# A four-layer graph network on one core: a tile turned through DRAM in layer 3, a recurrent step split by graph, another order of the tasks and dummy products

## The chip, the cores and the metric

The kernel runs on one core of a Trainium2 chip. The metric is the time of one execution on the device in microseconds (us), the median of the runs shown. The engines that matter are TensorE (PE, with its weight loads PEld), VectorE (DVE), ScalarE (ACT), GpSimd (POOL), and SyncE (SP), whose queue issues every DMA of this kernel.

## What is computed

64 graphs of 256 nodes with 256 features pass four residual layers, each `x = x + layer(relu(layernorm(x)), adj)`. All numbers are float32; the adjacency is int32.

```
layer 0  q, k, v = h@Wq, h@Wk, h@Wv in 8 heads of 32
         softmax(where(adj > 0, q@k.T / sqrt(32), -1e9)) @ v, then @Wo + bo
layer 1  Wh = h@W;  e = leaky_relu(Wh@a1 [:,None] + Wh@a2 [None,:])
         attention = softmax(where(adj > 0, e, -9e15), axis=1);  elu(attention @ Wh)
layer 2  three times:  m = h@weight[i];  aggr = A.T-sum of m over the edges
         h = GRU(aggr, h):  r, z = sigmoid(...);  n = tanh(i_n + r*h_n);  h = (1-z)*n + z*h
layer 3  f = h@W.T + b in 4 heads of 64
         logits = leaky_relu(s_src[i] + s_dst[j]), masked where adj != 1
         out = softmax(logits, over j) @ f
```

## The kernel before

**Tiling.** The graphs are taken two at a time, 32 pairs. A pair's x lives in one tile of 128 partitions x 1024 (four chunks of 128 nodes x 256 features: two per graph), loaded at the start and stored after layer 3. Six such x tiles exist, so several pairs are under way at once. Other working tiles come from pools with fixed numbers of slots (`SLOTS`, L324): 21 tiles "w4" of 4 KB per partition, 5 "w2" of half that size, 8 PSUM banks "ps", 8 DRAM tiles "turn" of 512 KB, 4 "turn2" of 256 KB.

**The order of the work.** Nothing runs in the order in which it is written. Each piece of work is a `Task` with one or more forms (an engine, an estimated time, and the instructions); `Plan.add` (L195) notes which tiles it reads and writes. A constant string `ORDER` (L48) holds, for every task, a rank and the form chosen. `Plan.order` (L240) sorts the tasks by rank, walks through them once with a small model of the engines (when each is free, how long a result takes to reach another engine, `latency` times 1.4 for a DMA), gives each tile the slot that comes free first, and emits the instructions. Every engine then works through its own list in that order, waiting for semaphores. Changing an estimate changes the slots given out; changing `ORDER` changes each engine's list. The planner also charges 0.19 us when TensorE changes the mode of its array: "full" 128x128, "rows" of 32 (layer 0's scores, L844), "columns" of 32 (layer 0's context, L896), and "halves" of 64 columns (layer 3's product, L1300).

**Transposes.** Layers 0, 2 and 3 need the normalized tile with features on partitions. `norm_relu` (L584) has two ways. One uses TensorE: eight transposes of 128x128 into two PSUM banks (L664), each bank then passed through relu to SBUF by ACT (L676) or DVE (L677). The other, `turn_rows` (L764), goes through DRAM: one DVE transpose of 32x32 blocks over the whole tile (L768), a store of 512 KB to a "turn" tile (L723) and four loads of 128 KB that bring the blocks back in turned places (L726), then relu from SBUF (L648 on ACT, L649 on DVE). `by_dma` (L580) decides: layers 0 and 2 go through DRAM for pairs 0 to 30, and so do the three results of layer 2's steps ("2m", L1199); layer 3 and the last pair use TensorE. Apart from that, the exponentials of layers 0 and 3 are turned through DRAM by `turn` (L732), except in layer 3 of the last pair (`turn_keys`, L737).

**Layer 2.** Each of three steps computes gates with 512-column products for both graphs of a pair at once (`gate`, L1117; the products at L1124): the new part of h (L1134, L1136), the messages along the edges (L1101), then reset, update and candidate (L1149, L1154, L1163, L1172, L1176) and the new state (L1181, L1187, L1192).

**Layer 3.** The features f come from TensorE (L1246); destination scores go through DRAM to all partitions (`to_all`, L923, its DMAs at L928 and L936); ACT forms the logits (L1277), DVE masks them and finds the row maximum (L792), ACT takes the exponential (L799). After `turn`, the product with f (L1300) leaves the result with features on partitions. For all pairs but the last it is turned back by a DVE transpose (L1316), a store (L1320) and four loads (L1323), then scaled by the softmax sum and added to x by 16 DVE instructions of 64 columns per pair (L1334).

Of the kernel before, what the change touches and what calls it, by code (L numbers as in the profile page):

```python
# [11 lines left out]
FP = mybir.dt.float32  # L12
# [25 lines left out]
class Task:  # L38
    __slots__ = ("pair", "forms", "form", "bufs", "rank", "stage", "mode", "before", "end", "engine", "latency")


class Plan:
# [3 lines left out]
    SLOW, SWITCH = 1.4, 0.19  # L46

    ORDER = (  # L48
        "c-rlI2Y_T%m3Ezb?|b*<S2=f8=iJki6U>kqh9FVNf`bxFxW-*vcSZDHRM1_+qO7>AxQa?rRz*hQNQMbaf?;y%?&;}R)m{1B{}wPamAa>TNTS"
        "m)-PKk1y?fvJ&iT%F&b^JSGxS-RKJ<7U64EsK?}%Y0r__{_Uj7&8U+e;ezYbn~=5t^|8eRr>NB1*mH>9AK9{<I<U8uk53z1K3{?Urxi6f5Qp"  # L50
        "L85YtP5wZZ@SSCI;`VY0Agr<EfaDCgryJGK(Ao(E2C;o?=fQTkzr5V#aIKFa#Nd>s5>pHWbHM_>$|64w^(2_*j$qy`J@LNQq%PQK<`58FlP~"
        "$<JEDo{#ESp7_z7CW5ce#tL#Wpf@eThz7NR=y5@}0kspJe)|$O2>umFYylNhQC@e^E0f2Te%2str2(qFGNjvbbF{ERFq&#gcA0UPGtUekhbK"
        "zCz59hn_{m1x->~fk2lAxkK5COxG4=@6cgSv;5{*V21VINSEKmd^d+9c365cS8qMSiO%HR#X)9F3MmcZz7~N&rF#&^iobfD~eh`*egbjDW`9"
        "1wS{JiI^V?IT=JRjmdV)g^7hzpaA%lfSSNr6;c5exo0VTkD-*FLK(XqA;2x$VwXE4A>5x~^YO*0(Ns-Z8EHf?cZ}|Ro=W?iIjO%@f|j(N{lF"
        "^(Ajq;fOlUfYEj(+LOfBDnTFVj;Q&WGwgD4zb1BRd<TA*t~%`kGt2w)}I5IoJfU%t^TWxRn?#&#&*@MA(e$GCUezY|mvYHL7g>}m7T`VRq?#"
        "a<*~S1$!06|SaI?rJwi9ylkKX#1j1Nx0A@quIKznsS=L2V;Z&PAbFBXrLcJR&!}8hnz5uH%%izMqC^snY$s33X}lK3a9*;8%pV-Ifm4%U)_x"
        "!v(Fa)2us26bgfXND^Q&Nztg2Q0e*rn0&ExS>iPJmXFqv@0JYL4h{#cZeLy;qL^qH+&|oLB3o4(bHBDH6%#>CNU<?50oe=H?IHP%m{&@H_nZ"
        "U!II>@i49iv=xMzdVQQZPr%aX5Pe47jt9<K967n%TJDNE!Q04f)RNPi=lS*54@PpFx3^R4Cro4H!p<EG+`(kG?#Y#x`{+E@56gMjq1B2~Um>"
        "bqF<vnA2P!fE}x;HW0G22i)-3=_a^+bB?is>pKB%xbhS3JwgIokd=nuCI}6&&Ax2&dP5A1tLC}#hTzXcZCs_7tZCo=q^JUd=C(oC*T6n%8ke"
        "l>02SQmwaBj8y?YmI-Oo-${sA|cZ=hX2c7ss^i;+lfk^n^dkter)^oGs=fUqDf<R~)X?u#Y<38>t42()L!R9}>PAmd&|I8F%S5_f)-5l?-Dh"  # L60
        "zNyzG?6ue0|v;yvR{sGjh+DCUMk!Vu48L<gtn@n+2LLn%tQQ^-F`@1V4n%!mTJ&GEW6w)9)wf84MWY}hpwOlKU&`+=Hsd!$aq9~?Z*EmxNbW"
        "}4d8}Lc|f{Gr(f(`bdn@K8TNoL!f_gv$7g0_)-?i@A(G?PgII8f7!&FR<g#Zn2q`h7=op{d_{({ZZ%ub)(S|M+XrrXs*PX2+9Evlc1!_qgt1"
        "N4^fN*JYqxHw^+)ZQF>`gNP!a^=|`JZ(Jp`?-XA*O{X6Ysf{hbzpiM=U3@lODV5W2FAmzpmdASmznV=R^DE+SjmuuP@c4r)22Zeeu5Ub@~~?"
        "?XF?#y4iM4Blxnrq?Kv|GjWuXTq78Zmjg1#<4AR+hE#BgxJxi!c^SkERc5(gN+v+gh{B?{!5+mTr`nlW&UUy3?)->Zt14E*2sas;m&@c{nGF"
        "OIA_N3M=XUHRVaW4dbf*-h*xMkE+XF)5tU4i}eGDFeD?NS}UA;6ie#sLj-;SckImx#jALdsG!5O1z9yhu^EZ8Bgc)0mtx@5dG?~&On35~Yk?"
        "F!gM9<z(aSaPM`VK=2S>;4@+<k2B8WcR3$)L*hIH6ZQ<hbVYKoW(5Gy3c3vEP*g;+SJn8W8Vv=nD;WMBR)=q(rCi2DG=^R2tOZ`u`d=U5e%K"
        "_nCY6W0BIaaqb~4dlR*}F%^L;U6q}a)y=IN@pi3we8Z0LG>?T01z{DVb=4*B~j9&c!20@v9u>~*AW6BewH@h|1cg}N;J@f9C{!AFkQgxiD*$"
        "^PR{VU%;^LM{i!4CSluby__bCSfAK=2afJ8N-=;DgpgYhb?P!|-k0%3ShCn6qoY7u*g^kBPLqujZsW4Njo_^!j$Bbi!%7S>jhZY6DmRbnq-~"
        "8T193rCIK@nMo)Rs<m>kW;PXIh(EpLnpcC!zt^2;7X|ysyls-;6rqmN;Zt`lLa$yhyY6!GlVfZ2u;Jb2cYai<7jBZzGeEi@iRTfpli52xo+p"
        "&{<^jcNALBWy4%O_G!Q<XC>)EK_sz>()XwU^B@<(>bj`qDy?qQ1_gz15(DN+ow5ex5daGpS0y<i{+qiMOUP@`I+W1JIRy|Le;$3qtBaSR4H5"  # L70
        "%`l4Z73(Z`rLLAo$P(4?lwK`=;QymOM632FArVCoiCDNauCgucT&#$Oc(7WOpFyTHLhB+t_wJ~Mx>benLqMGTNjfhALPho{a)*qFN;XT^JY2"
        "6G)_8S|M(aLT<gE{(KDZG=w10WX~tUS5HmIXCa&3iDqMTN$8&4gx6enX^)_w0&t=5AP~)`q{u|VjWq@P$Ipqd|^?<<XkT&JU2fE-C9((J)Is"
        "AcUfO-ha%f`MK@c?|G@r==~$37|%oxtM8z%xJew!o~FZk`3zXm1D`F7T$6)m;LRv;>^1DVGJq;PnFO2}Sq04DPsw2->2ayUu-L*>d!0_&$6_"
        "KQlUa%MuWzo~4(cDMl2$&W~XM5?~IkA6gfldEz<&RFO)i7=g{r;PCf_*MZ%s;WhGff$&UQM`66F$qGG)&VomvGw4C}gbM|n)z%9TBJgZ&hzk"
        "?Dy*`OEjXn!wjVHc(f#HUv+=C<`?hr9}Swz$lNfRec19{UOj++A`qBF?>7xDZ-(bL9_4FO7%HK=p%%pod?BW@5H<8|=AZQ~S4!_*|uW@U}Jd"
        "l7~1G|EL#LTR<UDR-Q5N`g}?;JoLvesYcTl?8EbXn>VVVumyz%1B_rT~0^btDL;=WB>bK4qx1^EnD`$$+hNUJGf{6=ubn_p>3XN`Xt%>#_=~"
        "ogO1&ajE?0&o|Hs6{NE3D-uY`UH&X4Vnjd#v6Lt)@`>wg?L_CvpTE=lT$Bnx^;)9@Ag2iPA8t{W8hvgJ`_E?a(eDm`JZRh63+`lmQtrMOR^@"
        "JB@NIUHx+VYfd`KQ;ymy|iahgJF5Q`Ver@~4L11Py3GyLnCyK$|j68PjrbZ2MD9E=YhM1s$MZUEsm6O|@$vY*8EYet_%5Om?oYmrrvh{U7@h"
        "Wa^a5K)>A6^o*f}05-_bpnwkD3F4^Z+H~3`36M~?ql1``6b#r!IF2qWLib~hrV|aIv<y*rk~<p8<`it`UX*Zbx|)mD5KdWL(2-Mi1S~UY1ff"
        "M6VXN>^otOp7!8Ik2+*h99YBHS6Xda}a?=lZt@(2ZD_jmNj4p&x)|M{Axe#0LgG6ZRtWEu&3`_}wrLLNBv>%aK<@-OFQyz`Em(sRB8$OX0Xb"  # L80
        "@O&!Ot~T5|Mb!)@BK#WqYyE&-7iK#^QMLcZOo0nbl>^#DV3(@cs}w6?X$<}M$8KxYLfhCTcEE?s#~%m^V!g6?1~B|A~H#GNa`F&X3x#wD^2P"
        "E>017*`b$a&f5bFxe+AhSP8!{L#ohmsyAykS+dS98ciYb9(Rz*?)i_&`pPdE@5_fX-(F{~vl3L?-pFJXbLW0tVgg`A%b|A<gkpb+-3VL3F#a"
        "yXCV_L~6up62T>EiDxXL*q-D-yU#PJc}yDu&%Sn3v_GBc{n7k<r?I?g%D|cSVK(k(ixp3e3fUgDE6q5y3%t5N4!}){dZL2?-~HIx7U3d0bjH"
        "i76I^W{~<C2BiH>3ho?qXI8F{XofUMgNp8jl(zB=lV`M;f=nqx&&N(h5JcSpFwMPN2r%ixFJNVTU;`KN{l|`?1Y)yRaV?6lKsh>aT+6IqJ_#"
        "O%(SxzMXKV&JX_)8CdU);QrXDw;Id|a;D=zvRp3dD2h$hqyr;s!2Mvb1n@Ew%6Q1F=eDT#lqb7rU~p!$;EQd?hb^LFlR%bZpJQ+d>sM2VMHy"
        "gUF;3ri`FawSd21njU>iM#!_0QYWTT#F8ZD2k{y*#}E}PtVys{Ts7?3QwU1v=~15=n|7719!B#3>O+k5ah{?G@=vT4>?cpG2}vVZg;ndN4)N"
        "&D_OIiKrO&u8uh4(5%MII6#o?~_-x-T-t&l^>lr_hw9&vCMevHAN8G%kk`**Pi?xP~!AlC6uc%>2Z`k7=P-E`6EFjsB%^VPH5mj=)Y3t?8qg"
        "Ko%#k7p>hp2`9&s_%;HSu_Ag2qwBa@co^e9oE9baEw&#cJ7*)rwKn(nm&);qtDIi(jsV2q?tBR!}xUj0AhafX=w;gYM?7O)(I}O}hX16`GLd"
        "`a}drpUSC08gKsO!uh7iFw9vB|MQqs!`;xUWwL$w7$e8Ow(L{g>M!gaLU@1Np+mE^&!A}y2d+!}{tujkkZ|RS<DcAPkX#6K+`4Y9%;h+l&xV"
        "aNr~d$gF*gE7!eC64ozaXXuQ-;IdXjPp)R0d|J0+ejxb`{!ehG=l=Z*z-o|9RA`uf&w@J09`T#svRMtf_tI{uiSJ;|V9=ohgR;WA{7BfHn-o"  # L90
        "bDrta$Yf@2G{gc+Qd0<A2&0G7fhJN!PNqm6Vmp?9iM1yhDYI2MHb|g8;`XPcwX`wZa~l5L%IY8Ze$K6Xklf>dhCcdio1dyo+dCQ7B`0O$@-O"
        ")n2}OS0Bdz=L;r1h%qfl9ld>Y#&sgo+a221bCIvziHSmm<Fb8$FM4H|Gp%?L}WvKgne1+}tG|jbvB5Q&UKCYC1DtevZkxU*cjp`_BB52u_$N"
# [190 lines left out]
def tile_adj_preln_d4(  # L283
# [100 lines left out]
    def buf(tag):  # L384
        return Buf(tag, tiles[tag])

    def w4():
        return buf("w4")
# [1028 lines left out]
```

## Time and profile before the change

| what | value |
|---|---|
| time, median of 3 runs | 3501.86 us (3501.18 to 3503.47) |
| the profiled execution: its time | 3501.53 us |
| the profiled execution: span from first to last instruction | 3499.7 us |
| TensorE busy | 3433.5 us, 98% of the span |
| DVE busy | 3078.1 us, 88% |
| ACT busy | 2522.0 us, 72% |
| POOL busy | 453.1 us, 13% |
| DMA, the core's queue | 749.98 MB, 69.3% of 16 engines' span |
| gate products, L1124, two groups | 2304 instructions each, 1071.2 and 1064.9 us |
| granted TensorE clock, mean | 0.993 |

How to read it: the page gives busy time of each engine, the span in 40 slices with the busy share in tenths, the DMA queues, the chain of work that ended last, and the costliest groups of instructions by line. A float32 matmul is recorded as two instructions. Matmuls overlap in the records, so the distance between the starts of two groups says how long one holds TensorE, rather than the duration of one record.

### The profile page before, as it was taken

How to read it: one execution, taken by the hardware profiler on the slowest of the kernel's cores; microseconds unless marked ns; L12 is line 12 of the kernel's file. 1: busy time of each engine (PE TensorE's matmuls, PEld its weight loads, DVE VectorE, ACT ScalarE, POOL GpSimd, SP SyncE). 2: the span in 40 equal slices, each digit the busy share in tenths (PEclk: the TensorE clock that was granted, in tenths of full speed). 3: DMA queues.
4: the chain of work that ended last, by engine and by line, in shares of the span. 5: the costliest groups of instructions: out<-in, count | busy, mean ns of one | idle time of the engine just before them, and what ended most of it. 6: DMA issues, size and time to landing. Idle time of an engine off the chain costs nothing.

```text
span 3499.7 us, 53732 instructions
## 1 busy us (share of the span) xinstructions
PE 3433.5 (98%) x14784; PEld 1931.6 (55%) x14784; DVE 3078.1 (88%) x9047; ACT 2522.0 (72%) x6739; POOL 453.1 (13%) x497
## 2 busy tenths in 40 slices
PE   8899999999999999999999999999999999999997
PEld 5555555555555555555555555555555555555554
DVE  8788998999999989999899888999889989889767
ACT  7756786766776777777767777778777768668545
POOL 1010110111111111111111111111011111011010
PEclk9999999999999999999999999999999999999998
DMA  8655877777677777777776777777677776576444
GB/s 287 209 150 167 248 240 217 224 229 228 212 217 233 226 222 235 223 225 225 218 230 215 228 227 216 235 230 234 214 228 216 234 224 218 183 220 201 155 131 136
DMA packets 596081, 753.41 MB, mean 215 GB/s; under 512 B 99012, under 2 KB 507076, under 8 KB 595780
## 3 DMA queue, kind: packets, MB, share of 16 engines
q1 hardware_dynamic: 595780, 749.98, 69.3%
q8 instruction: 118, 1.93, 0.2%
q14 instruction: 183, 1.50, 0.1%
HBM read 426.78 MB, written 314.59 MB: 212 GB/s over the span
## 4 chain that ended last, share of the span: by engine, by line
PE 64%; DVE 7%; DMA 3%; ACT 2%; issue 1%; SPq 1%; POOL 0%; DVEq 0%; ACTq 0%; POOLq 0%
PE ps L1124 37%; PE ps L823 4%; PE ps L1101 4%; PE ps L1246 3%; PE ps L844 3%; PE ps L1300 2%; PE ps L699 2%; PE ps L1031 2%; PE ps L896 2%; PE ps L1017 2%; PE ps L911 2%; DMA w<-turn 2%; DVE w L792 1%; DVE w L954 1%; DVE x L1334 1%
## 5 line engine op out<-in xcount | busy, mean ns | idle before, releaser
L1124 PE MATMUL ps<-w,whhT 128*128 128x512 f32 x2304 | 1071.2, 594 | 1.2 <-DVE mx L792 1.0
L1124 PE MATMUL ps<-w,giT 128*128 128x512 f32 x2304 | 1064.9, 593 | 0.0
L799 ACT ACTIVATE w<-w,mx 128x256 f32<-128x256 f32 x1536 | 759.2, 499 | 45.2 <-DVE mx L792 43.7
L1124 PEld LDWEIGHTS ps<-w,giT 128*128 128x128 f32 x2304 | 435.9, 190 | 534.5 <-issue 511.2
L1124 PEld LDWEIGHTS ps<-w,whhT 128*128 128x128 f32 x2304 | 430.4, 190 | 496.3 <-issue 451.4
L734 DVE STREAM_TRANSPOSE w<-w 128x1024 f32<-128x1024 f32 x380 | 466.4, 1234 | 45.2 <-ACT w L876 25.7
L417 ACT COPY w<-ps 128x512 f32<-128x512 f32 x431 | 244.2, 579 | 198.1 <-PE ps L1300 79.0
L792 DVE CUSTOM_DVE_ANT_0 w<-ps,mask 128x256 f32<-128x256 f32 x1024 | 370.8, 417 | 14.7 <-PE ps L844 12.6
L876 ACT ACTIVATE w<-w,rz 128x256 f32<-128x256 f32 x678 | 292.4, 498 | 88.4 <-DVE rz L869 85.1
L619 ACT ACTIVATE w<-x,rs 128x256 f32<-128x256 f32 x464 | 244.7, 591 | 93.3 <-DVE rs L611 88.9
L799 ACT ACTIVATION_READ_ACCUMULATOR w<-w,mx 128x1 f32 x1536 | 293.4, 191 | 0.0
L1181 POOL TENSOR_TENSOR w<-w,w 128x512 f32<-128x512 f32 x86 | 114.0, 1332 | 1147.9 <-PE ps L1124 368.4
L1277 ACT ACTIVATE w<-w,f 128x256 f32<-128x256 f32 x512 | 219.5, 499 | 16.1 <-DMA w<-row 10.0
L1101 PE MATMUL ps<-part,part 128*128 128x256 f32 x1536 | 228.8, 299 | 1.8 <-DVE part L1091 1.7
L605 POOL TENSOR_SCALAR rs<-mv 128x4 f32<-128x4 f32 x129 | 40.9, 317 | 1368.0 <-DVE mv L594 1301.1
L1149 ACT ACTIVATE w<-ps,brz 128x512 f32<-128x512 f32 x192 | 129.3, 677 | 123.1 <-PE ps L1124 113.4
L1101 PEld LDWEIGHTS ps<-part,part 128*128 128x128 f32 x1536 | 197.3, 190 | 32.1 <-issue 18.3
L792 DVE CUSTOM_DVE_ANT_0 w<-w,mask 128x256 f32<-128x256 f32 x512 | 196.4, 428 | 13.3 <-ACT w L1277 12.4
L1176 ACT ACTIVATE w<-w,bih_sb 128x512 f32<-128x512 f32 x192 | 136.5, 716 | 97.4 <-DVE w L1172 97.3
L592 DVE BATCH_NORM_STATS2 st<-x 128x6 f32<-128x256 f32 x512 | 189.1, 411 | 10.8 <-DMA x<-in_x_dram 8.2
L1163 ACT ACTIVATE w<-ps,brz 128x512 f32<-128x512 f32 x192 | 129.2, 677 | 75.5 <-PE ps L1124 73.1
L1154 DVE SCALAR_TENSOR_TENSOR w<-w,w 128x512 f32<-128x512 f32 x192 | 132.6, 692 | 44.4 <-ACT w L1149 28.1
(117 smaller groups left out, 5132.7 us busy)
## 6 DMA issues: line engine op xcount, KB each, us to landing
turn<-w SPq DMA_DIRECT2D x535, 512.0 KB
w<-turn SPq DMA_DIRECT2D x2140, 128.0 KB
w<-in_adj_dram SPq DMA_DIRECT2D x128, 512.0 KB
w<-row SPq DMA_DIRECT2D x64, 512.0 KB
x<-in_x_dram SPq DMA_DIRECT2D x64, 256.0 KB
out_dram<-x SPq DMA_DIRECT2D x64, 256.0 KB
turn<-w SPq DMA_DIRECT2D x62, 256.0 KB
w<-turn SPq DMA_DIRECT2D x248, 64.0 KB
```

Of the source, the lines that this page charges most:

```text
L417: (A, act(n), lambda: nc.scalar.copy(dst(), src())),
L592: nc.vector.bn_stats(st()[:, t, :], tok(xt())[:, t, :])
L619: nc.scalar.activation(tok(xn())[:, t, :], tok(xt())[:, t, :], func, bias=rs()[:, 1, t : t + 1], scale=rs()[:, 0, t : t + 1])
L734: add((V, dve(T * N), lambda: nc.vector.transpose(blocks(), blocks())), writes=[e])
L792: nc.vector.tensor_tensor_reduce(row, src, mask, scale, 3.0e38, ALU.add, ALU.min, mn)
L799: nc.scalar.activation(row(e, r), row(e, r), AF.Exp, bias=mn()[:, r : r + 1], scale=-1.0, accum_out=zs()[:, z0(r) : z0(r) + 1])
L823: mm(ps(), w[:, k, o * P : (o + 1) * P], wide(hT, k), start=k == 0, stop=k == 1)
L876: op(row, row, rz()[:, r : r + 1])
L1101: mm(ps()[:, o * N : (o + 1) * N], chunk_of(part(), h.mixed, c, o), tok(ams[g](), N)[:, c, :], start=i == 0 and c == 0, stop=i == 1 and c ...
L1124: mm(ps(), w[:, k, c0 : c0 + P], wide(src, k), start=n == 0, stop=n == 2 * len(terms) - 1)
L1176: (A, act(N2, 1), lambda o=o, hn=hn: nc.scalar.activation(at_o(hn, o), at_o(hn, o), AF.Tanh, bias=bih_sb[:, 4 + o : 5 + o])),
L1277: nc.scalar.activation(dst, src, AF.Prelu, bias=f()[:, t, D + h : D + h + 1], alpha=ALPHA)
```

## The change

The diff makes these edits; line numbers are those of the kernel before.

- `TURNED` gets "3": layer 3's normalized tile goes through DRAM for pairs 0 to 30 as in layers 0 and 2. For layer 0 the first pair now uses TensorE. (`EARLY` is 0, so the other branches named `early` are not taken.)
- Layer 3's product is cut into column tiles of 32, twice as many instructions, in mode "columns".
- After the turn back, the scaling is done by two DVE products of 256 columns per graph, in place in the turned tile, and the addition to x by one instruction of 512 columns per graph, on POOL or DVE. The layout of the turned tile changes with it.
- The addition of layer 0's bias to x (L811) may go to DVE as well as POOL.
- In the last pair's third step of layer 2 the gates, the update and the transposes to tokens are written per graph (256 columns) instead of for both.
- The planner's model of DMA is new: each transfer has a time on a shared DMA resource (`dma`), a latency, 1.2 us for landing, and at most eight are under way. Several other estimates are changed.
- Where the planner's model sees TensorE idle for over 1 us, after the first 20 us, and a PSUM bank is free, it emits dummy transposes of the identity into that bank, as many as fill half of the wait at 0.11 us each. Nothing reads them.
- `ORDER` is replaced by another string, for the changed list of tasks.

```diff
-    SLOW, SWITCH = 1.4, 0.19
+    SWITCH, LANDING = 0.19, 1.2
+    IDLE, FILL = 1.0, 0.5
...
+            if engine == "SP":
+                begin = max(begin, lanes[0])
+            if engine == "PE":
+                idle = begin - free.get("PE", 0.0)
+                spare = [slot for at, slot in slots["ps"] if at <= free.get("PE", 0.0)]
+                if idle > self.IDLE and spare and begin > 20.0:
+                    out.append(lambda n=int(self.FILL * idle / 0.11), slot=spare[0]: self.busy(slot, n))
+                    now = "full"
...
-            t.end, t.engine = begin + us + t.latency * self.SLOW, engine
+            if engine == "SP":
+                free["DMA"] = max(free["SP"], free.get("DMA", 0.0)) + t.dma
+                t.end, t.engine = free["DMA"] + t.latency + self.LANDING, engine
+                lanes = lanes[1:] + [t.end + 0.1]
...
+    def busy(slot, n):
+        for i in range(n):
+            nc.tensor.transpose(tiles["ps"][slot][:, 0:P], ident, ident)
...
-    TURNED = ("0", "2", "2m",)
+    EARLY, LATE = 0, 1
+    TURNED = ("0", "2", "3", "2m")
...
-        return l in TURNED and p < B // 2 - 1
+        if l == "2m":
+            return p < B // 2 - 1
+        return l in TURNED and (1 if l == "0" else EARLY) <= p < B // 2 - LATE
...
     def through_dram(e, eT):
-        add((SP, 0.6, lambda: nc.sync.dma_start(d(), e())), reads=[e], writes=[d], latency=4.6)
+        add((SP, 0.41, lambda: nc.sync.dma_start(d(), e())), reads=[e], writes=[d], latency=1.41, dma=1.36)
...
-                reads=[d], writes=[(eT, b)], latency=3.8,
+                reads=[d], writes=[(eT, b)], latency=2.04, dma=0.5,
...
-                (G, pool(2 * D), lambda g=g: nc.gpsimd.tensor_add(
+                either(0.0, lambda eng, g=g: eng.tensor_add(
...
+            split = p == B // 2 - 1 and l == NL - 1
+            hn = w4()
+            u = w4() if hT.mixed else hT
+            steps = [gated(l, hT, hn, u, g) for g in ((0, 1) if split else (None,))]
+            for new_part, _ in steps:
+                new_part()
             plan.stage = "2m"
             aT = messages(h)
+            for _, rest in steps:
+                rest(aT)
...
-                            mm(
-                                pso()[j * C3 : (j + 1) * C3, k * N : (k + 1) * N],
-                                f()[:, 2 * g + c, h * C3 : (h + 1) * C3],
...
+                            for r in range(0, C3, 32):
+                                mm(
+                                    pso()[j * C3 + r : j * C3 + r + 32, k * N : (k + 1) * N],
+                                    f()[:, 2 * g + c, h * C3 + r : h * C3 + r + 32],
...
-            add((PE, 1.75, product), reads=[*eT, (f, 2 * g), (f, 2 * g + 1)], writes=[pso], claims=[oT], mode="halves")
+            add((PE, 1.75, product), reads=[*eT, (f, 2 * g), (f, 2 * g + 1)], writes=[pso], claims=[oT], mode="columns")
...
-                            nc.vector.scalar_tensor_tensor(
-                                xh, ap, rz()[:, H3 * c + h : H3 * c + h + 1], xh, ALU.mult, ALU.add
-                            )
...
+                def divided(o=o, rz=rz):
+                    for j in range(2):
+                        oj = o().rearrange("p (j a y i) -> p j a y i", j=2, a=2, i=32)[:, j]
+                        rj = rz().rearrange("p (y j) -> p j y", j=2)[:, j]
+                        nc.vector.tensor_tensor(oj, oj, rj.unsqueeze(1).unsqueeze(3).to_broadcast([P, 2, 4, 32]), ALU.mult)
...
+                def to_x(eng, g=g, o=o):
+                    xa = xt()[:, g * N2 : (g + 1) * N2].rearrange("p (y a i) -> p y a i", y=4, a=4)
+                    eng.tensor_add(xa, xa, o().rearrange("p (a y i) -> p y a i", a=4, y=4))
+
+                add(either(0.0, to_x), reads=[o], writes=[(xt, g)])
```

In the split step, `gated` holds the former code of the gates and of the update, with the columns of one graph where g is given and of both otherwise.

## The prediction before the result

> **What bounds the kernel now.** I read the engine totals and slices first, then busy time by stage, then TensorE's order of time in a steady stretch and at the end.
>
> ```profile
> span 3499.7 us, 53732 instructions
> ...
> PE 3433.5 (98%) x14784; PEld 1931.6 (55%) x14784; DVE 3078.1 (88%) x9047; ACT 2522.0 (72%) x6739; POOL 453.1 (13%) x497
> ...
> PE   8899999999999999999999999999999999999997
> ...
> DMA  8655877777677777777776777777677776576444
> ```
>
> TensorE is busy for 98% of the span, and the slices below nine tenths are the first and the last. Busy matmuls overlap, so that figure alone doesn't prove a bound; the stages do (columns: stretch, length, busy us with counts for PE, PEld, DVE, ACT, POOL; granted clock, DMA share, GB/s):
>
> ```profile
> 100.00:125.00 25.00, 16.57 (x112) 9.47 (x105) 21.21 (x73) 15.43 (x48) 3.72 (x4) 0.80 0.82 246
> 1000.00:1100.00 100.00, 100.00 (x436) 55.49 (x435) 92.61 (x275) 74.81 (x201) 15.00 (x17) 1.00 0.77 232
> 2400.00:2500.00 100.00, 100.00 (x446) 56.77 (x445) 90.92 (x276) 76.41 (x201) 10.52 (x12) 1.00 0.72 225
> 3440.00:3460.00 20.00, 13.63 (x36) 6.42 (x35) 18.74 (x53) 15.28 (x48) 0.94 (x2) 0.82 0.42 147
> 3460.00:3480.00 20.00, 13.94 (x56) 8.44 (x55) 12.07 (x51) 6.29 (x17) 0.94 (x2) 0.67 0.65 192
> 3480.00:3500.00 20.00, 11.43 (x70) 7.08 (x69) 16.02 (x57) 11.88 (x39) 1.27 (x1) 0.84 0.38 130
> ```
>
> In the steady stretches TensorE has no idle at all, beside a DVE at 91 to 93% and a DMA share of about 0.75. So time taken out of TensorE's instruction stream there shortens the span one for one, as long as neither of the others takes over. At both ends it waits, and the clock drops to 0.67 to 0.84 over whole stretches.
>
> Idle summed from TensorE's order of time: 60 us, of which 25 before 150 us, 20 in the middle and 15 after 3420 us (the page's 3499.7 - 3433.5 = 66 agrees). One wait of TensorE leads its table of waits, and its longest part is the one at 107 to 116 us:
>
> ```profile
> PE ps L896 <- DMA w<-turn: 12.8, 4, 8.4
> ```
>
> Stream rates, in TensorE's order of time (start, length, line; length overlaps the next start, so I use differences of starts):
>
> ```profile
> 1026.01 1.15 PE L844 MATMUL ps<-w,w 32*128 32x256 f32 x16
> 1027.09 3.67 PE L1300 MATMUL ps<-w,f 128*64 128x256 f32 x32
> 1030.69 1.15 PE L844 MATMUL ps<-w,w 32*128 32x256 f32 x16
> ...
> 1061.48 1.88 PE L1124 MATMUL ps<-w,giT 128*128 128x512 f32 x4
> 1063.19 1.04 PE L664 MATMUL ps<-ident,w 128*128 128x128 f32 x8
> 1064.07 3.60 PE L1124 MATMUL ps<-w,whhT 128*128 128x512 f32 x8
> ```
>
> Eight layer-3 transposes (L664) occupy 1064.07 - 1063.19 = 0.88 us. Two row-tiled score groups cost 1.08 us each. The last pair's end:
>
> ```profile
> 3448.41 1.88 PE L1124 MATMUL ps<-w,giT 128*128 128x512 f32 x4
> 3453.00 2.36 PE L1207 MATMUL ps<-ident,w 128*128 128x128 f32 x8 [2.71 <-DVE w L1192]
> 3458.89 1.13 PE L664 MATMUL ps<-ident,w 128*128 128x128 f32 x4 [3.53 <-DVE w L625]
> 3460.70 3.89 PE L1246 MATMUL ps<-w3a,w 128*128 128x264 f32 x8 [0.69 <-ACT w L676]
> ...
> 3468.79 3.89 PE L1246 MATMUL ps<-w3a,w 128*128 128x264 f32 x8 [0.69 <-ACT w L676]
> ...
> 3480.34 3.27 PE L744 MATMUL ps<-ident,w 128*128 128x128 f32 x13 [0.17 <-ACT w L799]
> ```
>
> From the last gate matmul (ends 3450.3) to the end are 49.4 us, in which TensorE mostly waits. L1246 x8 takes 3.9 us here, against 3.56 us for x16 at 1072.67: half speed. What L744's transposes do to the clock is to be seen in two stretches of 1 us (same columns as before):
>
> ```profile
> 3481.00:3482.00 1.00, 1.00 (x7) 0.87 (x5) 0.97 (x3) 1.00 (x5) 0.00 (x0) 0.50 0.23 57
> 3483.00:3484.00 1.00, 1.00 (x7) 0.57 (x8) 1.00 (x4) 1.00 (x4) 0.00 (x0) 0.77 0.59 225
> ```
>
> The second mean, 0.77, puts the return to full speed at 3483.46, before the L1300 products start at 3483.54: 3.1 us of nothing but transposes restored it.
>
> **What the Trainium skill says.** "TensorE: Matmul & The Clock Gate", Part 1: about 3.4 us without activity halves the clock, about 3.4 us of activity restores it. The trace agrees: full until 2.5 us after the last gate, then 0.50 until about 3473, after 4.3 us of unbroken L1246 and L1300. The same page, Part 4, says that full clock "doesn't engage for transpose-mode". Here the trace disagrees: the return at 3483.46, and the start, where 28 transposes from 6.86 us take 0.2 us each and yet the first L514 products behind them, at 12.49, stream at full rate. The measurement decides: transposes count, and so may the dummies, which are transposes. "TensorEngine Tiling (Array Packing)", Key Properties: a change of tiling mode drains the array. The trace agrees: a gate group before a row or column group takes 1.81 us instead of 1.72, and a row group 1.08 where 8 x 0.107 (32-row matmuls, four at once, at the rate of L1124 by size) = 0.86, so about 0.3 us per visit.
>
> **The change part by part.**
>
> *Layer 3's normalized tile through DRAM.* Pairs 0 to 30 drop 8 transposes: 31 x 0.88 = 27.3 us off a saturated TensorE. Pair 0's layer 0 gets its 8 back (+0.9 at most, in the start where TensorE waits anyway; I keep +0.9). Net -26.4. What is added lies elsewhere: on DVE a 128x1024 transpose, 1.24 us (L768), per pair; two relus now read SBUF (0.42 on DVE by L649, 0.62 on ACT by L648) instead of PSUM (0.67 and 0.59). On SP one store and four loads, 0.34 + 4 x 0.43 by the issue medians = 2.1 us per pair, in an in-order queue where all later transfers stand behind their waits. On the DMA engines 30 turns more (31 - 1) on 535, each 512 KB out and in: 1.05 MB per pair on 753.4 / 32 = 23.5, +4.5%, so a share of 0.75 becomes 0.78 to 0.79. Latency rises: by the new planner's constants 4.4 us for the store and 5.2 for the loads, with the DVE transpose some 11 us in place of about 1.5. Layer-1 masks (L944) run from 115.6 to 3269.7 us, 31 periods of 101.7 us, and six x tiles let a pair live several periods; 10 us fit, if the order has them. That cover gone, TensorE waits: see the rivals.
>
> *Output of layer 3.* The 16 scaled adds of 64 columns per pair (L1334, 111.9 / 31 = 3.6 us) become four 256-column products (L1221's 0.415 is the nearest row: 1.7) and two 512-column adds (0.69 on DVE, 1.33 on POOL). The DVE sum per pair: -3.6 + 1.7 + 1.24 - 0.4 = -1.1 with adds on POOL, +0.3 with them on DVE; the bias add of layer 0, now free to go to DVE, adds up to 1.4. So -1.1 to +1.7 on 92.5 (91% of 101.7): DVE stays below 94% of the shorter period. I take zero for the time.
>
> *Column tiles in layer 3's product.* Twice the instructions, four at once instead of two. The two forms stream alike (L1300 x32 3.60, L896 x64 3.59 us). The worth is in mode changes: 326 in the order of time, some 0.15 us each, 49 us. Of about 36 visits in halves mode only two touch a column group; each one merged saves up to 0.3 us, 10 in all. Bounds -10 to 0; I take -2, because only the order decides and the trace doesn't show it.
>
> *Last pair's last step by graph.* The same matmul columns, but graph 0's update, transposes, statistics and layer-3 chain begin about half of the step's gates early (48 instructions x 0.43 / 2 = 10 us), while graph 1's gates run. In the 49.4 us tail graph 1 follows 8.1 us behind graph 0 (L1246 at 3460.70 and 3468.79), and halved vector work takes about 1.5 us off its start. The tail's DVE chain also loses some of L1334's 5.4 us. If graph 1 goes where graph 0 was, -8 and -1.5 and -2; I take -11, bounds -18 (if it also sheds graph 1's waits on DVE) and -4 (row transfers or ACT's exponentials late next).
>
> *The order.* 25 us at the start, of which the first 6.9 wait for weights and stay. DMA share there is 0.75 to 0.96, so part is transfer-bound. A removable wait is the 8.4 us at 107 us, and the half-speed groups behind it (L896 x32 4.2 against 1.9 us, L823 x4 2.45 against 1.72: 3 us). I take -6, bounds -14 and 0. Middle idle, 20 us: a new order removes old gaps and makes some; -5, bounds -15 and +10.
>
> *Dummy products.* Only where the planner sees over 1 us of idle, filling half: hidden by the wait if it is there. If the clock is at one half each takes 0.22 to 0.27 instead of 0.11 and fills the whole wait; queued behind are the real matmuls, then every evacuation waiting on them. If the clock is held, one graph's L1246 at the end falls from 3.9 to 1.8 us, and its transposes (L1207 x8 2.36 us, at the stream rate 0.88) by a half: 3 to 4 us on the path there, and up to 3 at the start. Bounds -7 and +4 (a dummy that runs on after the wait is over); I take -3.
>
> Sum on the profiled execution's 3501.5 (span 3499.7 + 1.8 around it, 0.3 below the median 3501.9): -26.4 - 2 - 11 - 6 - 5 - 3 = -53.4, so **3448 us**. What is late next is TensorE itself in the middle, then the row transfers and the exponentials at the end.
>
> **The rivals.**
> (a) *TensorE stays the bound; terms as above.* 3448, own range 3426 to 3468. Chance 0.68.
> (b) *Half given back.* Later tiles or a full DVE make new gaps in the middle. For: DVE at 91 to 93%, SP's queue waits long for DVE transposes. Against: TensorE had next to no such wait in 2,500 us. At 0.8 us a pair, 25 us: 3473. Chance 0.20.
> (c) *Slower: SP's order blocks.* The added store waits at the head of SP's queue for a late transpose; the keys of layers 0 and 2 behind it land late, and TensorE stops at L896. It decides from 53.4 / 31 = 1.7 us of new TensorE wait per pair; a stop of 2.1 us in each pair gives 65 - 53 = +12: 3513. For: L896 already waits for turned tiles, 8.4 us once. Against: four such waits in the whole run. Chance 0.06.
> (d) *The saved transposes were filler.* If TensorE's work moves into waits elsewhere, the 27 us come back as idle and only small gains are left that cancel: 3500. Steady stretches with no idle speak against it. Chance 0.06, 0.04 of it within 0.2%, 7 us either way, about what a measurement of this kernel can tell from no change.
>
> Faster by over 0.2% (below 3494.9): 0.68 + 0.20 + 0.02 = 0.90; within: 0.04; slower (above 3508.9): 0.06. The range: (a)'s low end 3426 and up to (b)'s late side, 3482, leaving (c), (d) and some of each edge out.
>
> **What would show it.** Right: L664 left with 32 instructions (8 each for pair 0's layer 0 and the last pair's layers 0, 2 and 3), TensorE still without idle between 600 and 3000 us, a mask period of about 100.8 us, the tail after the last gate nearer 38 than 49 us. Wrong: TensorE waiting on turned tiles or on L664's successors in steady stretches, a DVE above 95%, more than 326 mode changes. If the clock falls to one half at the end beside dummies, they are worth nothing.

## The result, and the profile after

The changed kernel takes 3446.65 us (median of 4 runs, 3445.75 to 3449.86) against 3501.52 us of the kernel before on the same chips (4 runs, 3497.84 to 3503.47): ratio 0.9846, 95% interval 0.9829 to 0.9863. The forecast was 3448, range 3426 to 3482. The profiled execution took 3446.51 us, with a span of 3444.7. Of the changed kernel the page shows:

```profile
span 3444.7 us, 55545 instructions
...
PE 3398.8 (99%) x15685; PEld 1907.4 (55%) x15685; DVE 3116.7 (90%) x8899; ACT 2456.2 (71%) x6614; POOL 455.0 (13%) x498
...
PE   8999999999999999999999999999999999999998
...
DMA  8846887887767878778777777787788777776446
```

TensorE's busy share is 99% now, and DVE's has risen to 90%: the span has shrunk by 55.0 us and DVE's work has grown from 3078.1 to 3116.7. Busy time by stage (same columns as before the change):

```profile
100.00:125.00 25.00, 24.22 (x116) 16.30 (x115) 24.09 (x81) 20.00 (x63) 0.00 (x0) 1.00 0.91 258
1000.00:1100.00 100.00, 98.64 (x433) 54.47 (x426) 90.57 (x265) 68.45 (x186) 14.72 (x16) 1.00 0.82 245
2400.00:2500.00 100.00, 99.53 (x471) 55.99 (x470) 93.23 (x265) 73.27 (x200) 11.74 (x13) 1.00 0.74 235
3400.00:3420.00 20.00, 16.84 (x151) 13.24 (x150) 17.50 (x57) 15.00 (x42) 1.67 (x3) 1.00 0.70 231
3420.00:3440.00 20.00, 15.26 (x157) 10.86 (x155) 16.36 (x49) 13.89 (x45) 5.21 (x4) 0.91 0.67 205
```

The stretch at 100 to 125 us, which had TensorE busy for 16.57 us at a clock of 0.80, has 24.22 us at 1.00. The steady stretches are full or nearly so, as before. The last two stretches are at 15 to 17 us of 20, at nearly full clock. What TensorE waited for, by the longest totals:

```profile
PE ps L515 <- DMA w<-in_L_gnn_weight_dram: 6.2, 1, 6.2
PE ps L922 <- ACT w L480: 3.5, 5, 1.2
PE ps L578 <- DVE mx L860: 2.3, 1, 2.3
```

The 12.8 us of waits for turned tiles at the context product are gone; the first wait for weights stays. The end, in TensorE's order of time (L443 are the dummies, L732 the normalized tile's transposes, L1361 the features, L812 the transposes of the exponentials):

```profile
3400.81 1.03 PE L1219 MATMUL ps<-w,giT 128*128 128x256 f32 x4
3401.68 0.60 PE L732 MATMUL ps<-ident,w 128*128 128x128 f32 x4
...
3406.39 2.67 PE L443 MATMUL ps<-ident 128*128 128x128 f32 x23
3410.97 0.87 PE L732 MATMUL ps<-ident,w 128*128 128x128 f32 x4 [1.91 <-DVE w L693]
3412.53 2.05 PE L1361 MATMUL ps<-w3a,w 128*128 128x264 f32 x8 [0.69 <-ACT w L744]
3414.41 2.67 PE L443 MATMUL ps<-ident 128*128 128x128 f32 x23
...
3422.92 0.33 PE L812 MATMUL ps<-ident,w 128*128 128x128 f32 x1 [1.33 <-ACT w L867]
...
3424.39 3.03 PE L812 MATMUL ps<-ident,w 128*128 128x128 f32 x13 [0.16 <-ACT w L867]
3427.22 1.12 PE L443 MATMUL ps<-ident 128*128 128x128 f32 x6
3428.27 1.93 PE L1416 MATMUL ps<-w,f 128*32 128x256 f32 x32
```

From the end of the last gate product to the end of the span it is 43.0 us (3401.7 to 3444.7), 49.4 before.

**Where the 55 us came from.** I split each span into three: the *stream*, that is every TensorE instruction at its back-to-back rate (0.4293 us for 512 columns in the full array, in proportion for fewer, a quarter or a half of that where four or two tiles run at once, 0.11 for a transpose and for the message products); the *idle* time that the trace shows before TensorE's instructions; and the *rest*, which holds mode changes, half-speed clock and waits short enough to disappear in overlapping records.

| us | before | after | difference |
|---|---|---|---|
| stream | 3308.7 | 3289.9 | -18.8 |
| idle before 170 us | 24.8 | 14.2 | -10.6 |
| idle in the middle | 19.6 | 17.1 | -2.5 |
| idle in the last 80 us | 15.9 | 6.3 | -9.6 |
| rest | 130.7 | 117.2 | -13.5 |
| span | 3499.7 | 3444.7 | -55.0 |

The stream is the count that was forecast: 240 transposes fewer (L732 has 32 left), 26.4 us, and 69 dummies more, 7.6 us. Most of the fall of the rest is the clock. The trace grants TensorE half of its clock for 50.4 us of the span before the change and for 13.5 us after it. Half of that time, counted only where TensorE is busy, is 17.3 us before and 4.8 us after: 12.5 of the 13.5 us.

The gain can also be placed. Take TensorE's products at their stream rates, without transposes and dummies: 3266.9 us in both kernels. The first 100 us of them are through at 149.4 us before the change and at 134.1 us after it, the first 3100 us at 3286.8 and 3239.9. So the start gained about 15 us, the middle 32 and the end 8, each known to some 4 us, as will be seen (x1_no_dummies).

The tables say where the time went, not what caused each part. The experiments have to do that.

### The profile page after: what moved, and what is told of

Same layout as the page of the kernel before. It is cut to its first block, busy times and chain, and to the rows that moved or that the text cites. A ratio compares the mean times of both kernels' runs of the same rounds, so it can differ in the third digit from the quotient of the medians.

```text
span 3444.7 us, 55545 instructions
## 1 busy us (share of the span) xinstructions
PE 3398.8 (99%) x15685; PEld 1907.4 (55%) x15685; DVE 3116.7 (90%) x8899; ACT 2456.2 (71%) x6614; POOL 455.0 (13%) x498
## 3 DMA queue, kind: packets, MB, share of 16 engines
q8 instruction: 125, 2.05, 0.3%
## 5 line engine op out<-in xcount | busy, mean ns | idle before, releaser
L1219 PE MATMUL ps<-w,whhT 128*128 128x512 f32 (+1 forms) x2328 | 1079.8, 591 | 2.2 <-DVE mx L860 1.6
L1219 PE MATMUL ps<-w,giT 128*128 128x512 f32 (+1 forms) x2328 | 1068.0, 588 | 1.9 <-ACT w L480 1.8
L480 ACT COPY w<-ps 128x512 f32<-128x512 f32 x455 | 256.0, 579 | 176.3 <-PE ps L1180 51.7
L954 ACT ACTIVATE w<-w,rz 128x256 f32<-128x256 f32 x674 | 296.1, 499 | 57.4 <-DVE rz L948 56.3
L687 ACT ACTIVATE w<-x,rs 128x256 f32<-128x256 f32 x388 | 207.7, 592 | 132.3 <-DVE rs L679 128.6
L1282 POOL TENSOR_TENSOR w<-w,w 128x512 f32<-128x512 f32 x96 | 127.1, 1328 | 1086.3 <-ACT w L1276 842.1
L1180 PE MATMUL ps<-part,part 128*128 128x256 f32 x1536 | 252.8, 312 | 2.4 <-DVE mx L860 1.4
L1276 ACT ACTIVATE w<-w,bih_sb 128x512 f32<-128x512 f32 (+1 forms) x194 | 136.8, 712 | 115.3 <-DVE w L1272 114.7
L860 DVE CUSTOM_DVE_ANT_0 w<-w,mask 128x256 f32<-128x256 f32 x512 | 199.7, 423 | 20.5 <-ACT w L1392 19.2
L1250 ACT ACTIVATE w<-ps,brz 128x512 f32<-128x512 f32 (+1 forms) x194 | 129.6, 673 | 107.0 <-PE ps L1219 85.7
L1264 ACT ACTIVATE w<-ps,brz 128x512 f32<-128x512 f32 (+1 forms) x194 | 129.8, 674 | 93.7 <-PE ps L1219 86.8
L1288 DVE SCALAR_TENSOR_TENSOR w<-w,w 128x512 f32<-128x512 f32 (+1 forms) x194 | 136.0, 704 | 20.0 <-ACT w L1264 11.0
```

Source lines behind the costliest of these rows:

```text
L480: (A, act(n), lambda: nc.scalar.copy(dst(), src())),
L687: nc.scalar.activation(tok(xn())[:, t, :], tok(xt())[:, t, :], func, bias=rs()[:, 1, t : t + 1], scale=rs()[:, 0, t : t + 1])
L860: nc.vector.tensor_tensor_reduce(row, src, mask, scale, 3.0e38, ALU.add, ALU.min, mn)
L954: op(row(e, r), row(e, r), rz()[:, r : r + 1])
L1180: mm(ps()[:, o * N : (o + 1) * N], chunk_of(part(), h.mixed, c, o), tok(ams[g](), N)[:, c, :], start=i == 0 and c == 0, stop=i == 1 and c ...
L1219: mm(ps()[:, 0:n], w[:, k, c0 : c0 + P], of(wide(src, k)), start=i == 0, stop=i == 2 * len(terms) - 1)
```

## The experiments

In every comparison the yardstick is the kernel before on the same chip. A difference from the changed kernel is that of the two ratios times 3501.5 us. Each ratio has an interval of about 0.0015 to 0.002 either way, so a difference of under some 8 us is not resolved by the ratios alone; where I lean on a smaller one I say what else supports it.

**Eight transposes back onto TensorE** (x3_transposes_back), in the features' first product:

```diff
             def product(t=t, ps=ps):
+                if t == 0 and not last:
+                    for i in range(8):
+                        nc.tensor.transpose(ps()[:, 0:P], chunk(hT, i // 4, i % 4), ident)
                 for k in range(2):
```

> The changed kernel with eight transposes more on TensorE in layer 3 of pairs 0 to 30; their result is overwritten unread. My theory (TensorE bounds the middle, its stream counts one for one): 31 x 0.88 = 27 us slower, 24 to 29, so about 3474. Rival, that the gain came from the order and the freed TensorE time is idle now: 0 to 8 us slower.

Measured: ratio 0.9912 (0.9897 to 0.9927), 23 us slower than the changed kernel. Its page:

```profile
span 3464.6 us, 56041 instructions
...
PE 3422.6 (99%) x15933; PEld 1934.6 (56%) x15933; DVE 3116.5 (90%) x8899; ACT 2455.9 (71%) x6614; POOL 454.5 (13%) x498
```

The span grew by 19.9 us for 27.2 us of stream; idle fell by 3.6 and the rest by 3.7. So TensorE's stream does bound the kernel, and the rival is out. Whether it counts one for one this dose can't tell: by the ratio, 23 us known to some 8 us, it may; by the spans a part of what was added lies in waits that were there anyway.

**Sixteen** (x11_sixteen_back), the same edit at t = 0 and t = 2:

> The changed kernel with sixteen transposes more per pair in layer 3, 31 x 1.76 = 54.6 us of TensorE stream; eight cost about 23. Theory A (the first share is partly absorbed by TensorE's own waits, then it counts one for one): 47 to 52 us slower than the changed kernel. Theory B (every added us counts three quarters to nine tenths, always): 40 to 47.

Measured: ratio 0.9977 (0.9968 to 0.9987), 46 us slower, known to some 7 us. That is twice the first dose, and 84% of the 54.5 us of stream added, with an interval that ends just short of one for one. It falls in the range of theory B, but theory A is not ruled out: by the spans of the profiled executions the first eight cost 19.9 us and the second eight 24.6.

**Fewer transposes in the kernel before** (x5_before_fewer). Three quarters of layer 3's turned tile are left stale in pairs 0 to 30:

```diff
                 for j, (k, t) in enumerate(chunks):
+                    if base == "3" and not fine and j > 0:
+                        continue
                     nc.tensor.transpose(ps()[:, j * P : (j + 1) * P], tok(xn())[:, t, k * P : (k + 1) * P], ident)
```

> The kernel before, in layer 3 of pairs 0 to 30 with two transposes instead of eight, so three quarters of the turned tile hold stale values; the order, all evacuations and no transfer are changed. My theory (removal from TensorE's stream alone gives the gain): 31 x 6 x 0.11 = 20.5 us faster than before, 17 to 21, so about 3481. Rival, that the freed time turns into idle unless the order is searched anew: 0 to 8 us faster.

Measured: ratio 0.9963 (0.9950 to 0.9976), 13 us faster, 8 to 18, for 20.5 us of stream. The profiled execution:

```profile
span 3484.1 us, 53360 instructions
...
PE 3409.6 (98%) x14598; PEld 1905.4 (55%) x14598; DVE 3080.3 (88%) x9047; ACT 2522.2 (72%) x6739; POOL 455.6 (13%) x497
```

Its idle is 68.7 us in all against 60.3: 8.4 us of the freed time came back as waits. So in an order not made for it, removal is worth about two thirds, between the two expectations. The interval reaches up to 85%, so this share is not told apart from the 84% of the doses.

**Layer 3's turn undone in the new order** (x12_no_turn3). The entries of `ORDER` for the turn's tasks go to TensorE's transposes, placed where the last loads were, and to the two relus right behind them; tasks not yet free to run are put off:

```diff
+        if skipped:
+            for i in range(4):
+                add((SP, 0.0, None), mode="ghost")
...
+                add((PE, 4 * TURN, turn), reads=[xn], writes=[banks[i]], claims=[hT])
```

> The changed kernel with layer 3's turn through DRAM undone: TensorE's eight transposes stand where the loads were, the two relus right behind them, everything else in the new order. Theory A (TensorE's stream costs about 23, and DVE, freed of the 1.24 us transpose, gives back about 10): 8 to 16 us slower than the changed kernel. Theory B (only TensorE counts): 19 to 27 slower. Theory C (the turn's worth is the order's): less than 5 slower.

Measured: ratio 0.9992 (0.9984 to 1.0001), 51 us slower, outside all three. TensorE's groups of transposes against identity:

```profile
L727 PE MATMUL ps<-ident,w 128*128 128x128 f32 x248 | 37.4, 278 | 6.2 <-DVE w L705 5.6 <-ACT w L699 0.3
L455 PE MATMUL ps<-ident 128*128 128x128 f32 x164 | 20.8, 282 | 0.0
```

Beside the 248 transposes wanted, the planner emitted 164 dummies (L455) in place of 69, for it saw new waits of TensorE in the middle; the stream is 37.7 us longer than in the changed kernel, idle 7.8, the rest 8.7, of which half clock in the middle makes 6.3. So this is not a clean undoing. It shows that the order does not suit the old form: put into it, with the dummies and waits that come along, the old form loses nearly the whole gain. Of the time that the turn alone is worth it says nothing.

**The turn's bytes** (x6_small_turn). The same number of transfers, with 128 columns of the tile stored and 32 of each block loaded; seven eighths of the turned tile are stale:

```diff
+            add((SP, 0.41, lambda: nc.sync.dma_start(d()[:, 0:P], e()[:, 0:P])), reads=[e], writes=[d], latency=1.41, dma=1.36)
```

> The changed kernel in which layer 3's new turn moves one eighth of its bytes, in the same number of transfers; the rest of the turned tile holds stale values. My theory (the added transfers are hidden): no difference, within 2 us. Rival, that the added 4.5% of DMA traffic holds TensorE up: 5 to 20 us faster than the changed kernel.

Measured: ratio 0.9835 (0.9815 to 0.9855), 4 us faster than the changed kernel, which is not resolved from none. The profiled span is 3.0 us shorter, with 2.7 us less idle. By the spans the added bytes cost a few microseconds at most. The ratios alone, known to some 9 us here, would leave room for the low end of the rival. The number of the transfers and the time until their data arrive are not tested: this run keeps as many transfers.

**Layer 3's old output form in the new order** (x7_old_output): the sixteen 64-column DVE instructions per pair again, with the old layout of the turned tile:

```diff
-                        nc.vector.tensor_tensor(oj, oj, rj.unsqueeze(1).unsqueeze(3).to_broadcast([P, 2, 4, 32]), ALU.mult)
...
+                        nc.vector.scalar_tensor_tensor(
+                            xh, ap, rz()[:, H3 * c + h : H3 * c + h + 1], xh, ALU.mult, ALU.add
+                        )
```

> The changed kernel with layer 3's output scaled and added as before, sixteen DVE instructions of 64 columns per pair, where the new form has four products and two adds. My theory (DVE is not the bound): 0 to 2 us slower, from the last pairs' end. Rival, that DVE at 90% and more is the next bound and its relief part of the gain: about 1.9 us more DVE work in each of 31 pairs, so 10 to 30 us slower.

Measured: ratio 0.9871 (0.9856 to 0.9886), 9 us slower, 1 to 17; its four runs, 3453.8 to 3457.3, lie above all four of the changed kernel.

```profile
span 3452.0 us, 55808 instructions
...
PE 3401.1 (99%) x15694; PEld 1909.0 (55%) x15694; DVE 3140.2 (91%) x9239; ACT 2454.8 (71%) x6614; POOL 411.7 (12%) x468
```

DVE's work is 23.5 us more, POOL's 43 less, and TensorE's stream the same to 1 us. The edit that was costed at nothing is worth about 9 us, a little under the rival's range.

**The new output form in the old kernel** (x10_before_new_output), with the additions on POOL:

> The kernel before with the new form of layer 3's output, two products and one POOL addition per graph, in its old order. DVE loses sixteen 64-column instructions per pair and gains four products, some 60 us in all. Theory A (DVE work costs TensorE waits, at about 8.8 us of time per 23.5 us of DVE work as the old output in the changed kernel showed): 10 to 23 us faster than before. Theory B (that loss came from late additions to x in the new order, not from DVE's load): 0 to 4 us faster.

Measured: ratio 0.9978 (0.9971 to 0.9985), 8 us faster, 5 to 10. That lies between the two theories: DVE's busy time fell only by 18.7 us (3059.4 against 3078.1). Eight for 18.7 is about the rate of the old form in the new order, nine for 23.5. The step from the busy time of one group of instructions to what DVE as a whole would be spared was too large. The swap itself is as expected, 111.9 us of L1334 for 55.9 us of products. But another group of DVE instructions, L954, which the edit doesn't touch, takes 138.2 us in place of 117.9. That leaves 17 us, which no single group shows; busy times of groups overlap in the records.

**DVE's load by itself** (x13_dve_dose), the transpose of layer 3's output done twice:

```diff
+                def out_blocks(oT=oT, e2=e2):
+                    for i in range(2):
+                        nc.vector.transpose(
```

> The changed kernel with the DVE transpose of layer 3's output done twice, 62 x 0.70 = 43 us of DVE work more and nothing else. Theory A (DVE's load counts at about 0.37): 16 us slower, 10 to 22. Theory B (DVE is not a bound, the old output form cost by its late additions): 0 to 4 us slower.

Measured: ratio 0.9909 (0.9894 to 0.9924), 22 us slower, 14 to 30. The page and the longest waits of TensorE that are new:

```profile
span 3465.6 us, 55596 instructions
...
PE 3403.2 (98%) x15685; PEld 1905.7 (55%) x15685; DVE 3155.9 (91%) x8961; ACT 2455.2 (71%) x6614; POOL 452.5 (13%) x498
```

```profile
PE ps L1180 <- DVE part L1138: 5.2, 5, 1.7
PE ps L1361 <- ACT w L716: 3.8, 3, 1.6
PE ps L1219 <- ACT w L480: 3.4, 3, 2.2
```

DVE's busy time grew by 39.2 us, the span by 20.9, so half of it counts, though DVE stands idle for 9% of the span. The new waits are short, 1 to 2 us each, at message products, features and gates, and they arrive through ACT as often as through DVE. TensorE's idle rose by 16.5 us, the rest by 4.4; the middle now has two stretches at half clock, 3.4 us each, and the changed kernel has none there.

**No dummies** (x1_no_dummies); the planner's slots stay as they were:

```diff
     def busy(slot, n):
-        for i in range(n):
-            nc.tensor.transpose(tiles["ps"][slot][:, 0:P], ident, ident)
+        pass
```

> The changed kernel without its dummy products, all else in place. My theory (transposes count as activity and hold the clock): 3 us slower, 1 to 6, and at the end the granted clock at one half again while L1361 runs, its x8 groups at 3.9 us instead of 1.9. Rival, that the dummies do nothing for the clock: no difference in time, within 1 us, and the same clock at the end with and without them. Rival, that they delay real work: up to 4 us faster.

Measured: ratio 0.9848 (0.9831 to 0.9864), 1 us slower than the changed kernel, not resolved; the 3 us of the forecast are not excluded either. The profiled execution is the slowest of the four, 3452.24 us where their median is 3446.05. It is 3.9 us late after 20 us of products and 4.5 us late at the last gate, where the two programs have run the same instructions: all 69 dummies stand after 3406 us. Only the end can be compared. Without dummies (line numbers are one less here):

```profile
3405.26 1.03 PE L1218 MATMUL ps<-w,giT 128*128 128x256 f32 x4
...
3410.40 0.60 PE L1321 MATMUL ps<-ident,w 128*128 128x128 f32 x4
3415.42 1.22 PE L731 MATMUL ps<-ident,w 128*128 128x128 f32 x4 [4.42 <-DVE w L692]
3417.33 3.60 PE L1360 MATMUL ps<-w3a,w 128*128 128x264 f32 x8 [0.69 <-ACT w L743]
3422.01 1.93 PE L1415 MATMUL ps<-w,f 128*32 128x256 f32 x32 [1.08 <-DMA w<-turn]
3429.27 4.51 PE L811 MATMUL ps<-ident,w 128*128 128x128 f32 x16 [5.32 <-ACT w L866]
3433.71 2.13 PE L1415 MATMUL ps<-w,f 128*32 128x256 f32 x32
```

The second features group, L1360 x8, takes 3.6 us; with dummies the same group takes 2.05. The granted clock (third number from the right, ahead of the DMA share and GB/s), without dummies:

```profile
3416.00:3418.00 2.00, 1.31 (x5) 0.81 (x5) 1.07 (x8) 1.32 (x4) 0.00 (x0) 0.50 1.07 328
3418.00:3420.00 2.00, 2.00 (x6) 1.59 (x5) 0.43 (x1) 1.41 (x7) 0.00 (x0) 0.50 0.92 331
```

and of the changed kernel, beside its dummies (first two), and in a stretch of sparse and then dense transposes (last two):

```profile
3412.00:3414.00 2.00, 1.47 (x7) 1.28 (x8) 0.90 (x5) 2.00 (x8) 0.00 (x0) 1.00 1.10 292
3414.00:3416.00 2.00, 2.00 (x18) 1.89 (x17) 1.47 (x5) 1.11 (x4) 0.00 (x0) 1.00 0.97 374
3424.00:3426.00 2.00, 1.84 (x9) 1.65 (x10) 0.83 (x5) 2.00 (x7) 0.00 (x0) 0.61 1.06 284
3426.00:3428.00 2.00, 2.00 (x12) 2.00 (x11) 2.00 (x10) 2.00 (x7) 0.00 (x0) 0.54 1.05 346
```

So the dummies do hold the clock here: 23 of them between 3406.39 and 3409, 23 more from 3414.41. In the stretch from 3424.39 to 3428.27 TensorE runs transposes only, and the mean of 0.54 in its second half puts the return to full clock at about 3427.8, before the next matmul. So the clock did fall to one half for 3.4 us in spite of 17 dummies at 3419.51, which the prediction had named as the sign that they are worth nothing. From the last gate to the end it is 43.0 us with dummies and 44.3 without. By these two executions, and measured from the last gate, the dummies let the exponentials' transposes (L812, here L811) begin 1.9 us earlier, but the product behind them only 1.0 us earlier. In between stand the six dummies at 3427.22, with no wait after them; without dummies the product follows the transposes at once. So about 1 us of the saving was most likely lost to dummies that ran ahead of a product that was ready.

**Halves again** (x2_halves), tiles of 64 columns in layer 3's product:

```diff
-                            for r in range(0, C3, 32):
+                            for r in range(0, C3, C3):
```

> The changed kernel with layer 3's product in tiles of 64 columns again, half the instructions, in the same order of tasks. My theory (both forms stream alike, the edit only saves mode changes where layer 0's context stands next to it): 0 to 4 us slower. Rival, that a change of column width is a mode change like any other and the new order has put many such neighbours together: 5 to 10 us slower. Rival, that fewer instructions are better: faster.

Measured: ratio 0.9849 (0.9835 to 0.9864), and a profiled span of 3444.6 us against 3444.7. Twice the instructions or half of them, it is the same time. Nor did the order use the common mode: counted in the order of time, the changed kernel has 337 mode changes and this run, with one mode more, 339. The kernel before had 326.

**No split at the end** (x4_unsplit). Graph 0's transposes to tokens wait for both graphs:

```diff
-                add((PE, 4 * TURN, tokens), reads=[(hT, (0, g)), (hT, (1, g))] if split else [hT], writes=[ps], claims=[h])
+                add((PE, 4 * TURN, tokens), reads=[hT], writes=[ps], claims=[h])
```

> The changed kernel in which graph 0's chain after the last recurrent step waits for both graphs, tasks that are not yet free to run being put off in the order; the gate products stay at 256 columns. My theory (the split lets graph 0 run ahead at the end): 9 us slower, 6 to 13, all of it after about 3385 us. Rival, that the end is set by the row transfers and exponentials in any case: 0 to 3 us slower.

Measured: ratio 0.9867 (0.9852 to 0.9882), 7 us slower, which the ratios alone don't resolve. On the same chip its four runs (3449.2 to 3455.0) lie above all four of the kernel with halves (3443.9 to 3446.9), 6 us by the medians.

```profile
3399.57 1.03 PE L1226 MATMUL ps<-w,giT 128*128 128x256 f32 x4
...
3403.54 2.67 PE L450 MATMUL ps<-ident 128*128 128x128 f32 x23
3407.74 0.87 PE L739 MATMUL ps<-ident,w 128*128 128x128 f32 x4 [1.53 <-DVE w L700]
3409.30 3.58 PE L1368 MATMUL ps<-w3a,w 128*128 128x264 f32 x8 [0.69 <-ACT w L751]
...
3417.62 0.87 PE L739 MATMUL ps<-ident,w 128*128 128x128 f32 x4 [1.79 <-DVE w L700]
3419.18 3.73 PE L1368 MATMUL ps<-w3a,w 128*128 128x264 f32 x8 [0.69 <-ACT w L751]
...
```

From the last gate (3400.4) to the end (3453.2) it is 52.8 us, in place of 43.0. At the last gate the run is not late, so all of the loss lies after it, as expected. Both features groups come after the gates now, and both run at half speed (3.6 and 3.7 us, 3.2 us more than at full clock) in spite of 23 dummies ahead of each. The waits left unfilled, 1.53 and 0.69 us and then 1.79 and 0.69, are no longer than those in the changed kernel's end, 1.91 and 0.69, where the clock held. So what decides whether a half-filled wait holds the clock stays open. How much of the 3.2 us reaches the end is not shown either.

**Pair 0 through DRAM** (x14_pair0_dram), its store and loads right behind the DVE transpose:

```diff
-        if by_dma(base, p):
-            eT = turn_rows(xn)
+        first = base == "0" and p == 0
+        if first or by_dma(base, p):
+            eT = turn_rows(xn, "extra" if first else "full")
```

> The changed kernel with pair 0's layer-0 tile turned through DRAM again, the store and the four loads right behind the DVE transpose in SP's queue, the rest of the order kept. Theory A (the start's shorter idle, 14 us for 25, hangs on that tile being ready early while x is loaded behind the weights): TensorE waits for it and the run is 6 to 11 us slower than the changed kernel. Theory B (the start's gain is the order's alone, and this tile has slack): 0 to 2 us slower.

Measured: ratio 0.9858 (0.9841 to 0.9874), 4 us slower, which the ratios don't resolve; the profiled span is 5.4 us longer.

```profile
25.29 5.95 PE L457 MATMUL ps<-ident 128*128 128x128 f32 x53
32.68 3.85 PE L918 MATMUL ps<-w,wq_sb 128*128 128x512 f32 x8 [1.44 <-ACT w L731]
```

and of the changed kernel:

```profile
26.20 3.60 PE L901 MATMUL ps<-w,wq_sb 128*128 128x512 f32 x8
```

L918, here, and L901 are the first projection: 6.5 us later in this run. The dummies (L457 x53) fill the wait for 6 us. Measured by TensorE's products, the run is 9.7 us behind the changed kernel when 100 us of them are through, and 4.9 us behind after 3100 us. So theory A's loss appears at the start, and half of it comes back in the middle. Two executions of the same instructions differ by 3 to 4 us at the start (x1_no_dummies), so this is a rough figure.

## Why the prediction was right, point by point

**TensorE bounds the middle: right, its one-for-one worth too high.** The stream fell by the 26.4 us forecast. The step that took "no idle at all" in the steady stretches for a bound "one for one" was somewhat too strong: in a fixed order the measured share is 84% (sixteen transposes added to the new kernel) or about two thirds (some removed from the old). By the first share the transposes are worth some 22 us. Of the signs named, L732 has its 32 transposes left and the end is nearer 38 than 49 us, if only just. Between 600 and 3000 us TensorE has 13.6 us of idle, and had 9.8 before. The mask period (L1023, 106.2 to 3206.7 us) is 100.0 us, shorter by 1.7 us where 0.9 was forecast; it also depends on where the order puts the masks.

**DVE "I take zero for the time": wrong, and the error has two sides.** The forecast placed DVE's work per pair within -1.1 to +1.7 us and below 94%, which held (38.6 us more in all, 1.2 per pair), and concluded that it costs nothing, which did not: 22 of 39.2 us of added DVE work turned into time, and 9 of 23.5 and 8 of 18.7 in the two runs on the output form. So the new output form is worth about 9 us that were not counted. By these rates the turn's own 1.24 us per pair, 38 us of DVE work, should cost 15 to 21 us; this is an estimate, since no run takes that transpose alone away.

**Added transfers hidden: right within what was measured**, 0 to some 4 us for the bytes of 30 turns more.

**Column tiles, -2: nothing measured**, and the order has more mode changes than before, the sign that was named as wrong for this step.

**Split, -11: right in mechanism, 7 measured.** The prediction counted the clock at the end under the dummies as well, and that may be the part counted twice. Next in line are the exponentials, as the prediction's last bound had it.

**Dummies, -3: right in the reading of the clock, the worth not resolved**, 1 us by the ratios and 1.3 by the two ends. Transposes count as activity; the clock was held through the features group. Of the 2 us saved on it about one was lost again to six dummies ahead of real work, the risk that the forecast had named. At the start, where up to 3 us were seen, the changed kernel has no dummies at all.

**The order, -6 at the start and -5 in the middle: too small at the start.** Idle at the start fell by 10.6 us, in the middle by 2.5, and by place the start gained about 15 us. Up to 10 of these hang on pair 0's tile going over TensorE, and half of that comes back later, so far as one profile tells. The 8.4 us wait for turned tiles is gone, and with it the 10 us at half clock from 111 us on. How much of the whole the new order is worth can't be separated, nor what the planner's new model of DMA adds by giving out other slots: the order is written for the new list of tasks, and x12 shows what happens when the two are taken apart.

The sum was right to 1.4 us, and in part by luck. The terms placed 6 us at the start, 33 in the middle (transposes, columns, the order's 5) and 14 at the end (split and dummies); the traces show about 15, 32 and 8. So the start was under by 9 and the end over by 6. In the middle the total fits, but not term by term: nearly the whole 26.4 us of stream came off the span there, although the doses say 22, and although 38.6 us more of DVE work should have cost 15 to 21 us by the rates above. The doses were given in fixed orders. That the new order made good the difference is likely, since TensorE's idle in the middle did not grow, but no run measures it.

## What to carry to other kernels

A trace in which one engine has no idle does not make every saving on it count in full, nor every cost on the next engine free: with TensorE at 98 to 99% and DVE at 88 to 91%, about 84% of TensorE's work and 40 to 55% of DVE's counted. DVE's dose shows how: 16.5 of 20.9 us came as many short waits of TensorE. Why TensorE's counts less than in full is not shown; about half of what was missing in the first dose came out of its visible idle. Measure both rates with a dose of useless work before costing an edit at nothing. These rates hold for a fixed order of the work; a new order can absorb what a dose says must be paid. And an order that was written for one form of the work makes a poor test bed for another form: undoing a part within it overstates that part.

## What the runs showed of the hardware

Transposes alone brought TensorE's clock back to full (3.1 us of them before the change, 3.4 us after it), against what was expected from the Trainium skill's "TensorE: Matmul & The Clock Gate", Part 4. At the start the change shows within the transposes themselves: in the kernel before they follow each other every 0.213 us from 6.86 us on and every 0.11 us from 12.2 us on.

These times are not thresholds. In both traces half clock comes in stretches of 3.41 us or two, three or six times that, unless the span's end cuts them. And 3.9 us of unbroken products from 3460.70 us in the kernel before did not end one, where the prediction found the trace in agreement with some 3.4 us of activity. Waits half filled with transposes held the clock in one ending (two stretches of 23 dummies beside waits of 1.9 and 0.6 us) and not in another, with waits of 1.5 and 1.8 us.

Layer 3's product with 32-column tiles and 64-column tiles takes the same time, 3444.6 us in the span with 64 columns and 3444.7 with 32, which has 1024 matmul instructions more.
